# Reading a weight-mixing stage's bases two at a time, 8 KB to a partition

## The chip, the cores and the metric

The kernel runs on one core of a Trainium2 chip. The metric is the device time of one execution in microseconds (us). The core has five engines that run side by side and wait for each other by semaphores: TensorE (PE in the profile; its weight loads are PEld), VectorE (DVE), ScalarE (ACT), GpSimd (POOL) and SyncE (SP). SP and POOL also issue the DMA transfers, which the core's 16 DMA engines carry out.

## The reference

Two layers of a graph network with 625 nodes of 512 features. The change lies in the first of the two graph convolutions of the first layer, in one einsum:

```python
def rgcn_gate_layer(x, row, col, edge_type, basis, att, gate_w, root, bias):
    w = jnp.einsum('rb,bio->rio', att, basis)      # att [2, 30], basis [30, 512, 512]
    x_j = x[col]
    msgs = []
    for r in range(NUM_RELATIONS):                 # 2 relations
        gate = jax.nn.sigmoid(x_j @ gate_w[r, :, 0])
        msgs.append(gate[:, None] * x_j @ w[r])
    msg = jnp.where((edge_type == 0)[:, None], msgs[0], msgs[1])
    agg = jax.ops.segment_sum(msg, row, num_segments=x.shape[0])
    return agg + x @ root + bias

h = jax.nn.relu(rgcn_gate_layer(x, row, col, edge_type, basis1, att1, gate_w1, root1, bias1))
out = rgcn_gate_layer(h, row, col, edge_type, basis2, att2, gate_w2, root2, bias2)
```

So 30 bases of 512 x 512 numbers in f32 (31.5 MB) are summed into two weight matrices, one for each relation, with 30 factors each. The second convolution does the same with its own 30 bases. Around these stand a linear attention, expert layers and, in the second layer, graph attentions.

## The kernel before, in words

**Mixing layer one's bases on TensorE.** `mix_bases_1` builds 32 steps `q`, each a pair of functions, `load` and `step`. The bases are in two groups of 15 (`BGROUPS`); the even `q` take the first group, the odd ones the second, and each two consecutive `q` cover 32 rows `i` of the bases. `loaded` (L320) takes a tile `basis` of 128 partitions x 4 x 512 from a pool of three (`basis_pool`), and issues four transfers on SP (L325). Transfer j brings 8 rows (`BROWS`) of each of 15 bases into column block j: partition 8b + c holds row c of base b, so 120 partitions are filled with 2 KB each. `step` (L328) then runs four matrix products (L334), one for each column block. Their stationary operand is `att1[g]`, 120 x 32, which holds att in the places (8b + c, 2c + r): the product sums over the bases and puts row c, relation r into PSUM row 2c + r. Four blocks fill the four quarters of one PSUM bank, the second group is added to the first, ACT copies the bank to `stage` (L338), and POOL issues four stores (L341) from `stage` into `wmix`, the mixed weights, with 8 partitions x 2 relations x 512 each.

**The order of work.** It is written out by hand: inside `manual_schedule`, PE and SP run in program order. `mix(n)` loads and runs n steps. The program starts with two steps; then for each group of 11 edge columns (`count_group`, one-hot products on PE that count edges) it runs one or two steps and one piece of the linear attention (`key`, `value`, `query`), and after the last group come the steps left over. The last four steps alternate with the first slices of layer two (the string `plan`, `DPDPDPDP` and then D's): a "D" loads three quarters of one base of layer two into a tile of the same pool (L356 on SP) and DVE adds it with its factor (L367). The first quarter of each of layer two's bases comes through `ring`, loaded by POOL's queue (L356), and is added by DVE. `load_w` (L79) brings `wk`, `wv`, `wq` and `root` on SP in between. When the last step of layer one is done, `root_products(1)` and `root_products(3)` run, and then `messages(1, ...)` multiplies the nodes with `wmix` (L138).

**Transfers.** SP's transfers use eight semaphores in turn, and one that reuses a semaphore waits until the transfer before it on that semaphore has landed.

Of the kernel before, what the change touches and what calls it, by code (L numbers as in the profile page):

```python
# [21 lines left out]
D = 512  # L22
# [6 lines left out]
BROWS = 8  # L29
# [16 lines left out]
def kernel(ctx: ExitStack, tc: tile.TileContext, A, out: bass.AP):  # L46
    nc = tc.nc
# [126 lines left out]
    def mix_bank():  # L174
        return banks[2]()
# [135 lines left out]
    def mix_bases_1(wpool):  # L311

        w = wpool.tile([128, 2, KD * D], F32, name="wmix")
        src = A["L0_gnn_basis1"].rearrange("b (i c) o -> i b c o", c=BROWS)
        acc = [None]

        def loaded(q):  # L320
            i0, g = 4 * (q // 2), q % 2
            n, b0 = BGROUPS[g], sum(BGROUPS[:g])
            bt = basis_pool.tile([128, KD, D], F32, name="basis")
            for j in range(4):
                nc.sync.dma_start(bt[:BROWS * n, j, :], src[i0 + j, b0:b0 + n])  # L325
            return bt

        def step(q, bt):  # L328
            i0, g = 4 * (q // 2), q % 2
            k = BROWS * BGROUPS[g]  # L330
            if g == 0:
                acc[0] = mix_bank()
            for j in range(4):
                nc.tensor.matmul(acc[0][32 * j:32 * j + 32, :], att1[g][:k], bt[:k, j, :],  # L334
                                 start=(g == 0), stop=(g == 1))
            if g == 1:
                sg = stage_pool.tile([128, D], F32, name="stage")
                nc.scalar.copy(sg, acc[0])  # L338
                for j in range(4):
                    k, p0 = (i0 + j) // 16, 8 * ((i0 + j) % 16)  # L340
                    nc.gpsimd.dma_start(w[p0:p0 + 8, :, k * D:(k + 1) * D], sg[32 * j:32 * j + 16, :])  # L341

        return w, [(lambda q=q: loaded(q), lambda bt, q=q: step(q, bt)) for q in range(32)]

    class Added:
# [91 lines left out]
    b0 = 0  # L437
    for n in BGROUPS:
        k = BROWS * n
# [19 lines left out]
    for i in range(2):  # L459
        g = rowsA.tile([128, KD, 32], F32, name=f"gwp{i}")  # L460
# [46 lines left out]
    def gates_of(psg):  # L507
        gate = rowsA.tile([P, NT, 2], F32, name="gate")
        nc.scalar.activation(gate.rearrange("p t r -> p (t r)"), psg[:P, :2 * NT], AF.Sigmoid)
        return gate  # L510

    wm1, steps = mix_bases_1(wpool)

    def mix(n=1):
# [1066 lines left out]
```

## Time and profile before

| | |
|---|---|
| median of three runs | 981.48 us (976.95 to 981.51) |
| the profiled execution: its time, its span | 975.78 us, 974.0 us |
| busy: PE, DVE, ACT, POOL | 890.9, 514.2, 304.1, 142.8 us |
| basis transfers of layer one (L325) | 128 of 240 KB, from 3.3 to 215.4 us |
| products on them (L334) | 256, of which 224 in `mix` banks, 650 ns each |
| end of the last of these products | 221.8 us |

The span runs from the first to the last instruction; the run's time is a little longer. The times of the profile's views are counted from the start of the span. In the page, a group of instructions is named by its line, its engine, its operation and its tiles (output<-inputs). "Busy" of PE includes pipelined matrix products, so a busy PE is not PE at its peak. The DMA share is the mean busy share of the 16 DMA engines, and a transfer is cut into packets, of which each belongs to one engine.

### The profile page before, as it was taken

What the parts mean: (1) busy time and instruction counts of PE and PEld (TensorE: products, weight loads), DVE (VectorE), ACT (ScalarE), POOL (GpSimd) and SP (SyncE); (2) the same over time, 40 slices, a digit from 0 to 9 for tenths busy, and PEclk for the clock granted to TensorE, in tenths of its full rate; (3) what the DMA queues carried; (4) which work ended last, traced back from release to release, by engine and by line L of the source; (5) the groups of instructions that cost most, each with busy time, mean ns of one, the idle gap of its engine ahead of it and who ended that gap; (6) DMA issues with size and microseconds to landing.
All of it is one profiled execution on the core that took longest, in us unless ns stands there. A gap on an engine that the chain in (4) does not pass through costs nothing. (4 is left out here: it accounts for less than half of the span.)

```text
span 974.0 us, 10135 instructions
## 1 busy us (share of the span) xinstructions
PE 890.9 (91%) x3606; PEld 488.1 (50%) x3606; DVE 514.2 (53%) x980; ACT 304.1 (31%) x508; POOL 142.8 (15%) x223
## 2 busy tenths in 40 slices
PE   3898899979999999789969999999988899997997
PEld 1333234534474448767735655555544554444543
DVE  7778694566889723422254632233355754566320
ACT  2566475611120021111125432322243442311310
POOL 6644231110000200330020000000000000011310
PEclk9999999999999999799989999999999999997999
DMA  8899997575487920889831111212210104020001
GB/s 243 244 280 259 251 248 185 169 196 196 135 285 230 334 87 2 265 292 331 281 120 56 44 43 47 81 46 87 86 64 27 61 1 128 10 77 2 0 6 47
DMA packets 70842, 135.06 MB, mean 139 GB/s; under 512 B 9298, under 2 KB 11485, under 8 KB 70787
## 3 DMA queue, kind: packets, MB, share of 16 engines
q1 hardware_dynamic: 61554, 114.19, 38.3%
q0 software_dynamic: 9232, 20.16, 6.9%
q8 instruction: 31, 0.51, 0.2%
q14 instruction: 25, 0.20, 0.1%
HBM read 123.37 MB, written 8.85 MB: 136 GB/s over the span
## 5 line engine op out<-in xcount | busy, mean ns | idle before, releaser
L367 DVE SCALAR_TENSOR_TENSOR wmix<-basis,att,wmix 128x1536 f32<-128x1536 f32 x58 | 101.4, 1811 | 12.8 <-DMA basis<-in_L_gnn_basis_dram 12.8
L133 PE MATMUL ps<-y1T,wh 128*128 128x512 f32 (+1 forms) x256 | 74.5, 440 | 1.5 <-DVE hm L1281 1.0
L138 PE MATMUL ps<-hm,wh 128*128 128x512 f32 (+1 forms) x256 | 71.7, 433 | 0.0
L233 DVE TENSOR_SCALAR os<-iota,edges,wbits 125x626 bf16<-125x626 f16 x123 | 49.9, 469 | 26.6 <-PE tail L236 26.5
L138 PE MATMUL ps<-wmix,xnT 128*125 128x512 f32 x140 | 61.9, 592 | 0.0
L235 PE MATMUL main<-os,odg 125*128 125x512 bf16 x165 | 48.7, 381 | 11.9 <-ACT os L231 6.4
L133 PEld LDWEIGHTS ps<-y1T,wh 128*128 128x128 f32 x256 | 41.1, 190 | 33.8 <-issue 30.6
L138 PEld LDWEIGHTS ps<-hm,wh 128*128 128x128 f32 x256 | 39.7, 191 | 30.7 <-issue 30.7
L341 POOL DMA_DIRECT2D wmix<-stage x64 | 37.0, 581 | 98.2 <-ACT stage L338 98.1
L334 PE MATMUL mix<-basis,att 120*32 120x512 f32 x224 | 42.4, 650 | 8.8 <-DVE att L450 5.6
L659 PE MATMUL ps<-z,counts 125*125 125x512 f32 x200 | 48.3, 397 | 0.6 <-PEq L644 0.6
L1291 DVE TENSOR_TENSOR acc<-acc,sg 128x625 f32<-128x625 f32 x15 | 12.2, 811 | 64.1 <-ACT sg L1289 64.1
L367 DVE SCALAR_TENSOR_TENSOR w<-ring,att,w 128x512 f32<-128x512 f32 x58 | 40.8, 752 | 9.8 <-DMA ring<-in_L_gnn_basis_dram 9.8
L1281 DVE TENSOR_SCALAR hm<-ps,bh 128x625 f32<-128x625 f32 x32 | 27.7, 867 | 31.4 <-PE ps L133 31.4
L138 PEld LDWEIGHTS ps<-wmix,xnT 128*125 128x125 f32 x140 | 26.3, 188 | 33.8 <-issue 33.0
L1279 ACT ACTIVATE hm<-ps,bh 128x625 f32<-128x625 f32 x32 | 25.0, 782 | 55.4 <-PE ps L133 55.4
L138 PEld LDWEIGHTS ps<-xgT,w1e 128*128 128x128 f32 x320 | 38.1, 199 | 7.7 <-ACT xgT L1021 7.7
L659 PEld LDWEIGHTS ps<-z,counts 125*125 125x125 f32 x200 | 36.5, 185 | 10.8 <-issue 2.2
L138 PE MATMUL ps<-xgT,w1e 128*128 128x128 f32 x320 | 39.9, 285 | 1.2 <-ACT xgT L1021 1.2
L138 PE MATMUL ps<-w2e,hTe 128*128 128x512 f32 x80 | 37.5, 595 | 3.0 <-DVE hTe L1030 3.0
L636 ACT ACTIVATE z<-ps,gate 125x512 fp32r<-125x512 f32 x20 | 13.7, 687 | 79.9 <-PE ps L138 79.9
L133 PE MATMUL ps<-xnT,wq 128*128 128x113 f32 (+1 forms) x128 | 36.5, 438 | 2.0 <-DVE cT L74 1.2
(358 smaller groups left out, 1522.6 us busy)
## 6 DMA issues: line engine op xcount, KB each, us to landing
basis<-in_L_gnn_basis_dram SPq DMA_DIRECT2D x128, 240.0 KB
basis<-in_L_gnn_basis_dram SPq DMA_DIRECT2D x30, 768.0 KB
w1e<-in_L_ffn_W_dram SPq DMA_DIRECT2D x10, 1024.0 KB
w2e<-in_L_ffn_W_dram SPq DMA_DIRECT2D x10, 1024.0 KB
ring<-in_L_gnn_basis_dram POOLq DMA_DIRECT2D x30, 256.0 KB, 7.9
wh<-in_L_gnn_Wh_dram SPq DMA_DIRECT2D x4, 1024.0 KB
xd<-stage POOLq DMA_DIRECT2D x12, 256.0 KB, 6.4
b2row<-in_L_ffn_b_dram SPq DMA_DIRECT2D x10, 256.0 KB
```

The costliest lines, as they stand in the source:

```text
L133: nc.tensor.matmul(ps[:m, lo:hi], l, r[:, lo:hi], start=(i == 0), stop=(i == len(pairs) - 1))
L138: nc.tensor.matmul(ps, l, r, start=(i == 0), stop=(i == len(pairs) - 1))
L233: nc.vector.tensor_scalar(os_, iota, edges[:, 0, c:c + 1], wfield[:, c:c + 1], op0=OP.is_equal, op1=OP.mult)
L235: nc.tensor.matmul(main0, od[:, c - c0, :], os_[:, :BANK], start=c == 0, stop=c == NE - 1)
L334: nc.tensor.matmul(acc[0][32 * j:32 * j + 32, :], att1[g][:k], bt[:k, j, :], start=(g == 0), stop=(g == 1))
L341: nc.gpsimd.dma_start(w[p0:p0 + 8, :, k * D:(k + 1) * D], sg[32 * j:32 * j + 16, :])
L367: nc.vector.scalar_tensor_tensor(w[:, r, :], self.tiles[b], c, w[:, r, :], op0=OP.mult, op1=OP.add)
L636: nc.scalar.activation(hi[:, t, :], ps[:P], AF.Copy, scale=g)
L659: nc.tensor.matmul(ps[:P], l, r, start=first and i == 0, stop=last and i == len(pairs) - 1)
L1279: nc.scalar.activation(hm[:, m, :], ps[:, :N], AF.Relu, bias=b)
L1281: nc.vector.tensor_scalar(hm[:, m, :], ps[:, :N], b, 0.0, op0=OP.add, op1=OP.max)
L1291: nc.vector.tensor_add(acc, acc, sg)
```

## The change

A transfer brings two bases instead of fifteen, and 32 neighbouring rows of each instead of 8. Row 4c + i of the 32 lies in partition c, block i, so that a partition gets four neighbouring rows, 8 KB in one piece. Two bases fill 16 partitions; seven such transfers and one of a single base fill the tile's 120 partitions. The tile's shape, the pool, the products and their operand stay. Block j now holds the rows 4c + j in place of 8j + c, so the stores put the mixed rows into every fourth partition.

```diff
-        src = A["L0_gnn_basis1"].rearrange("b (i c) o -> i b c o", c=BROWS)
+        src = A["L0_gnn_basis1"].rearrange("b (q c i) o -> q b c i o", c=BROWS, i=4)
         acc = [None]
 
         def loaded(q):
-            i0, g = 4 * (q // 2), q % 2
+            g = q % 2
             n, b0 = BGROUPS[g], sum(BGROUPS[:g])
             bt = basis_pool.tile([128, KD, D], F32, name="basis")
-            for j in range(4):
-                nc.sync.dma_start(bt[:BROWS * n, j, :], src[i0 + j, b0:b0 + n])
+            for b in range(0, n, 2):
+                m = min(2, n - b)
+                nc.sync.dma_start(bt[BROWS * b:BROWS * (b + m)], src[q // 2, b0 + b:b0 + b + m])
             return bt
 
         def step(q, bt):
-            i0, g = 4 * (q // 2), q % 2
+            g = q % 2
             k = BROWS * BGROUPS[g]
...
             if g == 1:
                 sg = stage_pool.tile([128, D], F32, name="stage")
                 nc.scalar.copy(sg, acc[0])
+                k, p0 = q // 8, 32 * (q // 2 % 4)
                 for j in range(4):
-                    k, p0 = (i0 + j) // 16, 8 * ((i0 + j) % 16)
-                    nc.gpsimd.dma_start(w[p0:p0 + 8, :, k * D:(k + 1) * D], sg[32 * j:32 * j + 16, :])
+                    nc.gpsimd.dma_start(w[p0 + j:p0 + 32:4, :, k * D:(k + 1) * D], sg[32 * j:32 * j + 16, :])
```

## The prediction

> **What bounds the kernel now.** I read the windows view by stage first, then the waits of the first 222 us, then the basis tile's rows, and last the DMA view of two short stretches, because the change only re-cuts transfers.
>
> ```profile
> 50.00:100.00 50.00, 44.21 (x221) 17.55 (x221) 41.47 (x75) 31.36 (x43) 19.49 (x38) 0.97 1.00 270
> 100.00:150.00 50.00, 44.88 (x210) 17.30 (x204) 38.93 (x68) 27.23 (x38) 15.94 (x27) 1.00 0.99 250
> ```
>
> After the window come its length, then busy time of PE, PEld, DVE, ACT, POOL, granted clock, DMA share and GB/s. In the stage that mixes layer one's bases all 16 DMA engines are taken (share 1.00), at 250 to 270 GB/s, and PE is busy nine tenths of the time. So both are close to being the bound here. After 222 us the bases of layer one are done and PE carries the end (91% of the span).
>
> ```profile
> SPq L325 <- PE mix L334: 44.5, 12, 6.8
> SPq L325 <- DMA basis<-in_L_gnn_basis_dram: 22.8, 20, 5.6
> PEld mix L334 <- DMA basis<-in_L_gnn_basis_dram: 15.9, 19, 2.7
> PEld ps L334 <- DMA basis<-in_L_gnn_basis_dram: 9.3, 7, 2.5
> PE ps L334 <- DMA basis<-in_L_gnn_basis_dram: 6.2, 5, 3.0
> PE mix L334 <- DMA basis<-in_L_gnn_basis_dram: 3.1, 4, 1.8
> ```
>
> Total, times, longest, in the first 222 us. TensorE and its weight loads stood 34.5 us (15.9 + 9.3 + 6.2 + 3.1) for a basis tile: that is the most that better transfers could win. SP's queue is not full: it waits for a free buffer or for a transfer to land.
>
> ```profile
> L325 SPq DMA_DIRECT2D basis<-in_L_gnn_basis_dram x128: 835/838/1225, 3.3 to 215.4; - x128
> L356 SPq DMA_DIRECT2D basis<-in_L_gnn_basis_dram x30: 367/368/563, 179.5 to 320.7; - x30
> ```
>
> Issue time on SP in ns (least, median, most). A transfer whose source counts in two steps (15 bases, 8 rows) and whose tile counts in one (120 partitions) costs SP 838 ns; one whose two sides count alike costs 368.
>
> How many of the 16 engines does one transfer use? The DMA view of 115.2 to 120.8 us, where basis transfers alone move data, tells:
>
> ```profile
> DMA packets 816, 1.49 MB, mean 266 GB/s; under 512 B 90, under 2 KB 90, under 8 KB 816
> q1 hardware_dynamic: 816, 1.49, 99.0%
> basis<-in_L_gnn_basis_dram SPq DMA_DIRECT2D x6, 240.0 KB
> ```
>
> 726 packets carry rows; at 120 rows each that is 6.05 transfers. The other 90 packets are small, 14.9 for a transfer: I read them as one closing packet from each engine that took part, so fifteen engines carry a transfer whose source has 15 outermost steps. The stretch of 803 to 816 us shows what a transfer on few engines does:
>
> ```profile
> DMA  0002350332422333333333333333333300004967
> DMA packets 640, 1.27 MB, mean 98 GB/s; under 512 B 20, under 2 KB 20, under 8 KB 640
> bb<-in_L_gnn_b_dram SPq DMA_DIRECT2D x1, 250.0 KB
> bb_b<-in_L_gnn_bsk_dram SPq DMA_DIRECT2D x1, 250.0 KB
> g<-in_L_gnn_g_dram SPq DMA_DIRECT2D x1, 250.0 KB
> be<-in_L_gnn_be_dram SPq DMA_DIRECT2D x1, 250.0 KB
> ```
>
> Four rows are loaded into 125 partitions, issued within 1.5 us of each other. They end with 20 small packets, five each: 5 is the largest number up to 16 that divides 125. And the DMA line stays at 3 tenths, 5 of 16 engines, for ten microseconds: the four do not spread over the idle eleven engines, they queue on the same five. What one engine gives:
>
> ```profile
> 689.50:692.00 2.50, 2.50 (x10) 1.34 (x9) 0.87 (x1) 0.38 (x1) 0.00 (x0) 1.00 0.32 131
> 808.00:813.00 5.00, 5.00 (x13) 2.19 (x12) 2.19 (x4) 0.58 (x1) 1.27 (x1) 1.00 0.33 128
> ```
>
> Last two columns: share and GB/s, both on five engines; the first has rows of 4 KB, the second of 2 KB. That is 26.2 and 25.6 GB/s an engine. Row size is worth 2%, no more.
>
> **The change, part by part.**
>
> *The loads.* The bytes stay: 32 tiles of 120 rows of 8 KB, 31.5 MB. Four transfers of 240 KB for a tile become seven of 128 KB (two bases) and one of 64 KB (the fifteenth basis). In a pair the source, read from `src[q // 2, b0 + b:b0 + b + m]`, counts 2 bases, then 8 stretches of 8 KB; the tile counts 16 partitions. The Trainium skill ("DMA: Bandwidth & Descriptors", section "Why a DMA increments its semaphore by 16 and not by 1") says that a transfer is split along the outermost count of each side, over the largest number of engines up to 16 that divides both, and that on the hardware queues these are the lowest-numbered ones. The rows above agree as far as they reach (15 for 15 and 120; 5 for 125 and 125, always the same five), but 15 also follows from the 120 partitions alone, so no row here tells "both sides" from "the partitions". By the partitions a pair would use 16 engines and lose nothing; by both sides it uses **2**, and 224 pairs queue behind one another on the same two engines while fourteen idle. I take 2, as the rule is stated for both sides and nothing in the trace contradicts it.
>
> Then the stage is bound by those two. Each carries half of every pair, 224 x 64 KB = 14.68 MB, and one row of each single (8 partitions, 8 engines), 32 x 8 KB = 0.26 MB: 14.94 MB at 25.6 GB/s is 584 us. They also carry their sixteenth of all else that moves meanwhile: the ring slices of layer two 7.9 MB, four weight loads 4.2, four slices of 768 KB 3.1, the wmix stores 2.1, x 0.8: 18.1 MB / 16 = 1.13 MB, 44 us. The sum is 628 us from the first issue at 3.3 us: the last tile lands at about 631 us.
>
> The same skill page ("Why small descriptors are slow") charges each packet some 3 fixed cycles beside one for each 32 bytes: 67 for 64 at 2 KB, 259 for 256 at 8 KB, so 8 KB rows would run 3.4% faster. The trace's 2% from 2 to 4 KB is of that size. By the rule the 584 us become 565; with the measured 2 KB rate 584. I keep 584 and let the rule set the low end.
>
> *SP's issues.* 256 instead of 128. A pair still counts differently on its two sides, so between 368 and 838 ns, and I take 838: 224 x 0.838 + 32 x 0.34 (a row load with equal sides, the 281 to 294 ns of `bb` at the end and up) = 199 us, against 107 now. Spread over 628 us this lies beside the transfers and costs nothing; if the transfers were quick it would fill the stage (rival two). Behind SP's waiting loads stand `wk`, `wv`, `wq`, `root` and the first `slices` loads, in program order, so these come late as well, but their users on PE (`key`, `value`, `query`, root_products) stand between mix steps that wait longer. POOL's `ring` loads meet the same two engines with a sixteenth of their rows, and DVE's `w20` steps wait for that; 18 us a tile cover it.
>
> *TensorE.* Before, product j of a tile needed transfer j alone; now each needs all eight. The last tile's four products (593 ns each) then run one after another behind the last landing, where now one does: 2 us later than before. Elsewhere they hide in the wait: a tile takes 7 x 2.56 = 18 us to arrive (64 KB at 25.6 GB/s each), and PE was busy 182.6 us of 12 to 221 us, about 6 us for each of the 32 tiles.
>
> *The way back.* ACT's copy is unchanged; the four `wmix` stores from POOL have the same count, bytes and shape (8 partitions, 2 rows of 2 KB), with a partition step of 4. Nearest row: 550 ns of issue, 6.7 us to land. Bounds: a microsecond less or more for each landing; they have 37 us between groups, and the last four lie beside the 7.5 us of root products:
>
> ```profile
> 220.73 1.04 PE L334 MATMUL ps<-basis,att 120*32 120x512 f32 x2 [0.51 <-DMA basis<-in_L_gnn_basis_dram]
> 229.49 1.02 PE L138 MATMUL ps<-wmix,xnT 128*125 128x512 f32 x2
> ```
>
> I take 0, range -1 to +2 us.
>
> *What comes after.* The last product of layer one's bases ends at 221.8 us now; 752 us follow, nearly all PE, in the same order, with the slices of layer two loaded on all 16 engines as before. Only what precedes the last tile waits.
>
> **The sum.** 631 + 3 (landing, products) + 752 = 1386 us of span, 1388 with the 1.8 us that lie between this execution's span (974.0) and its time (975.78). The median of the runs shown, 981.48, is 0.6% above the profiled one; I don't add that.
>
> **The rivals.**
>
> *Two engines (chance 0.87).* The forecast. Its own range: 27 GB/s an engine and 30 us of other traffic give 1342; 24 GB/s, 47 us and 10 us of gaps between tiles give 1440.
>
> *Sixteen engines, SP the bound (0.07).* Should the split follow the partitions, 199 us of basis issues and some 6 us of others must pass through SP before the last tile, of 215 us that pass now, with hardly a wait allowed. Each wait for a buffer then adds: 975 to 1010, say 985. Against it: the rule; for it: 838 ns where counts differ.
>
> *The stage gets shorter (0.06): faster.* One mechanism: enough engines and issues at 368 ns. Layer one's 31.5 MB need 144 GB/s to keep the present 218 us, which at 25.6 is six engines; from there on the split costs nothing, and 8 KB rows give back half of the 34.5 us of waits: about 960. The point that decides is the number of engines a pair uses: under six it loses, above it wins.
>
> **How the numbers follow.** The two-engine case holds 0.87 and ends slower. Of the second 0.01 is faster, 0.02 same, 0.04 slower; all of the third is faster. About 0.5% (5 us) is what a measurement of this kernel can tell from no change. That makes 0.07, 0.02 and 0.91. The range 1335 to 1440 holds nearly all of the two-engine case and leaves the others out.
>
> **What would show it.** Right: from 5 to about 630 us the DMA line at 1 to 2 tenths (2 of 16 is 0.13, plus ring and slices) and near 60 GB/s; PE at a third or less of busy time there; waits of L334 for basis of hundreds of us; 3,840 rows of 8 KB in q1 in place of 15,360 of 2 KB; after it the old 752 us. Wrong: a DMA share above 0.4 in the stage means more engines; an SPq without waits means the issue bound; an L325 median near 368 would spoil the 838.

## The result and the profile after

The changed kernel takes 1416.76 us (median of four runs, 1415.68 to 1419.91) against 979.22 us for the kernel before on the same chip: 1.4475 times as long, with a 95% interval of 1.442 to 1.4529. The forecast was 1388 us, in a range of 1335 to 1440. The span of the profiled execution is 1413.9 us, of which TensorE is busy 932.6 us (890.9 before).

The first view is part 2 of the page after: the span in 40 slices of 35.3 us, with the busy tenths of PE, the granted clock, the mean share of the DMA engines and what they moved.

```profile
PE   0203332343335353614999989979999998999798
PEclk9855556666577685756999989989999999999899
DMA  3442211112111113324378158841122220031001
GB/s 112 129 142 81 82 57 58 56 58 79 58 58 59 58 55 97 91 73 140 130 270 300 62 159 288 298 153 60 30 60 60 89 75 30 30 89 59 1 1 37
```

Slices 6 to 15 (176 to 530 us) stand at one tenth and 55 to 59 GB/s, but for one of 79 in which a weight also arrives: for 350 us the transfers keep little more than two of the sixteen engines busy. PE works about a third of that time, and from slice 20 (from 670 us) it runs as before. The windows view (length, busy PE, PEld, DVE, ACT, POOL, granted clock, DMA share, GB/s) gives the same for two stretches, and the DMA view for the second of them:

```profile
200.00:250.00 50.00, 15.36 (x57) 5.15 (x58) 5.05 (x10) 6.95 (x10) 2.22 (x4) 0.60 0.15 57
250.00:300.00 50.00, 18.61 (x75) 7.06 (x73) 9.69 (x19) 11.77 (x16) 2.22 (x4) 0.67 0.15 57
```

```profile
DMA packets 515, 2.84 MB, mean 57 GB/s; under 512 B 154, under 2 KB 154, under 8 KB 186
q1 hardware_dynamic: 386, 2.69, 13.4%
basis<-in_L_gnn_basis_dram SPq DMA_DIRECT2D x19, 128.0 KB
basis<-in_L_gnn_basis_dram SPq DMA_DIRECT2D x2, 64.0 KB
```

In 50 us SP's queue moved 2.69 MB. Two singles are in it, whose rows go to eight engines, so about 0.1 MB of theirs went to other engines than the first two. The rest, 2.59 MB in 50 us on two engines, is about 26 GB/s an engine, at the 25.6 to 26.2 that the two stretches of before gave.

The kernel feels it as one wait. Three rows of the waits of the first 680 us (engine, tile, line, what it waited for: us in total, times, longest), one of SP's queue, and the row of the basis tile's loads (issue time on SP in ns, least, median, most):

```profile
PE mix L336 <- DMA basis<-in_L_gnn_basis_dram: 352.7, 27, 27.3
DVE os L233 <- PE tail L236: 331.9, 14, 37.0
...
PE ps L336 <- DMA basis<-in_L_gnn_basis_dram: 59.4, 4, 18.3
```

```profile
SPq L327 <- DMA basis<-in_L_gnn_basis_dram: 428.8, 208, 4.3
```

```profile
L327 SPq DMA_DIRECT2D basis<-in_L_gnn_basis_dram x256: 278/605/4835, 3.3 to 636.4; - x128
```

(L325, L334 and the like of before are two lines further down here; in some experiments they are one or three.) PE stands 412 us (352.7 + 59.4) for bases, where PE and its weight loads together stood 34.5 us before. SP stands 428.8 us for earlier transfers to land, so its own issuing holds nothing up. DVE's 331.9 us are only handed on, as the edge counts wait for PE, and PE for the bases between them. The end of the stage, in the timeline of PE:

```profile
657.12 1.93 PE L336 MATMUL ps<-basis,att 120*32 120x512 f32 x8 [18.29 <-DMA basis<-in_L_gnn_basis_dram]
...
659.46 4.05 PE L661 MATMUL ps<-root,xnT 128*125 128x512 f32 x8
...
667.43 4.88 PE L138 MATMUL ps<-wmix,xnT 128*125 128x512 f32 x11
```

The messages begin at 667.43 us, against 229.49 before. What follows takes 746.5 us here and 744.5 there. All of the loss but 2 us lies ahead of that point.

### The profile page after: what moved, and what is told of

The parts are those of the page before. It is cut to its first block, busy times and chain, and to the rows that moved or that the text cites. A ratio compares the mean times of both kernels' runs of the same rounds, so it can differ in the third digit from the quotient of the medians.

```text
span 1413.9 us, 10434 instructions
## 1 busy us (share of the span) xinstructions
PE 932.6 (66%) x3606; PEld 502.0 (36%) x3606; DVE 512.0 (36%) x980; ACT 303.6 (21%) x508; POOL 138.6 (10%) x223
## 2 busy tenths in 40 slices
DMA packets 58108, 135.09 MB, mean 96 GB/s; under 512 B 8081, under 2 KB 10268, under 8 KB 54210
## 5 line engine op out<-in xcount | busy, mean ns | idle before, releaser
L336 PE MATMUL mix<-basis,att 120*32 120x512 f32 x224 | 54.2, 1059 | 352.7 <-DMA basis<-in_L_gnn_basis_dram 352.7
L233 DVE TENSOR_SCALAR os<-iota,edges,wbits 125x626 bf16<-125x626 f16 x123 | 47.2, 446 | 332.2 <-PE tail L236 331.9
L336 PEld LDWEIGHTS mix<-basis,att 120*32 120x32 f32 x224 | 6.2, 140 | 375.2 <-issue 207.5
L138 PE MATMUL ps<-hm,wh 128*128 128x512 f32 (+1 forms) x256 | 71.7, 433 | 0.0
L340 ACT COPY stage<-mix 128x512 f32<-128x512 f32 x14 | 8.2, 585 | 291.7 <-PE mix L336 258.0
L138 PE MATMUL ps<-wmix,xnT 128*125 128x512 f32 x140 | 61.9, 592 | 0.0
L138 PEld LDWEIGHTS ps<-hm,wh 128*128 128x128 f32 x256 | 39.7, 191 | 30.7 <-issue 30.7
L336 PE MATMUL ps<-basis,att 120*32 120x512 f32 x32 | 7.7, 1058 | 59.4 <-DMA basis<-in_L_gnn_basis_dram 59.4
L138 PE MATMUL ps<-wk,xnT 128*125 128x512 f32 x80 | 43.8, 700 | 0.0
L138 PE MATMUL ps<-wv,xnT 128*125 128x512 f32 x80 | 42.6, 683 | 0.0
L133 PE MATMUL ps<-xnT,wq 128*128 128x113 f32 (+1 forms) x128 | 40.1, 468 | 1.9 <-DVE cT L74 1.1
L661 PE MATMUL ps<-root,xnT 128*125 128x512 f32 x80 | 40.0, 647 | 0.8 <-DMA root<-in_L_gnn_root_dram 0.8
L138 PE MATMUL ps<-w2e,hTe 128*128 128x512 f32 x80 | 38.4, 607 | 2.4 <-DVE hTe L1032 2.4
L138 PEld LDWEIGHTS ps<-xgT,w1e 128*128 128x128 f32 x320 | 37.3, 195 | 7.5 <-ACT xgT L1023 7.5
```

What stands on the lines that cost most here:

```text
L133: nc.tensor.matmul(ps[:m, lo:hi], l, r[:, lo:hi], start=(i == 0), stop=(i == len(pairs) - 1))
L138: nc.tensor.matmul(ps, l, r, start=(i == 0), stop=(i == len(pairs) - 1))
L233: nc.vector.tensor_scalar(os_, iota, edges[:, 0, c:c + 1], wfield[:, c:c + 1], op0=OP.is_equal, op1=OP.mult)
L661: nc.tensor.matmul(ps[:P], l, r, start=first and i == 0, stop=last and i == len(pairs) - 1)
```

## The experiments

Theory: a transfer is split along the outermost count of both sides, over the largest number of engines up to 16 that divides both, so a pair uses two engines and layer one's bases need their time. Rivals: the split follows the partitions and SP's issues bind; or the long rows or the whole-tile waits cost the time; or the order of work on DVE, which the scheduler rearranged, does.

One table first, by which all runs can be read. "Small" is the count of packets under 512 bytes in part 2 of each page. The other transfers have 7,377 or 7,378 of them in every kernel here, and the rest are the closing packets of layer one's transfers, read as in the prediction as one for each engine taking part. On that reading the number of engines can be counted; it comes out whole for every kernel, and the 2 of the changed kernel agrees with its rate above. "Start" is the first product on `wmix` (L138), and "after it" the span less that.

| kernel | layer one's transfers | small packets | engines | start, us | after it | time, us |
|---|---|---|---|---|---|---|
| before | 128 | 9,298 = 7,378 + 128 x 15 | 15 | 229.5 | 744.5 | 979.22 |
| after | 224 + 32 | 8,081 = 7,377 + 224 x 2 + 32 x 8 | 2 | 667.4 | 746.5 | 1416.76 |
| e1 rows outermost | 224 + 32 | 9,425 = 7,377 + 256 x 8 | 8 | 326.5 | 746.7 | 1073.99 |
| e2 three bases | 160 | 7,857 = 7,377 + 160 x 3 | 3 | 494.0 | 749.5 | 1245.27 (one run) |
| e3 five bases | 96 | 7,857 = 7,377 + 96 x 5 | 5 | 350.7 | 749.8 | 1102.29 (one run) |
| e4 fifteen bases | 32 | 7,857 = 7,377 + 32 x 15 | 15 | 256.2 | 745.4 | 1002.42 |
| e9 two halves | 64 | 8,337 = 7,377 + 64 x 15 | 15 | 239.8 | 747.7 | 988.94 |
| e12 issues doubled | 256 | 11,217 = 7,377 + 256 x 15 | 15 | 261.5 | 743.7 | 1006.46 |

The times without a mark are medians of four or more runs. The kernel before ran beside each group of experiments with a median of 977 to 979 us. No kernel here beats it.

**e1: the same pairs, rows outermost.** Only the order of the source's counts differs from the changed kernel: the same 224 pairs into the same 16 partitions, with the same 8 KB rows. The rows of a pair now lie in a different order in the partitions, so the operand `att` is built to match.

```diff
-                nc.sync.dma_start(bt[BROWS * b:BROWS * (b + m)], src[q // 2, b0 + b:b0 + b + m])
+                nc.sync.dma_start(bt[BROWS * b:BROWS * (b + m)],
+                                  src[q // 2, b0 + b:b0 + b + m].rearrange("b c i o -> c b i o"))
```

> The transfers of the changed kernel with their 16 rows in another order: the same two bases, the same 16 partitions and rows of 8 KB, 224 pairs and 32 singles on SP, but the source counts 8 row stretches first and 2 bases second (partition 2c + b in place of 8b + c; the mixing operand is permuted to match). Two-engine theory (the outermost count of the source sets the engines): 8 engines a pair, 31.46 MB / (8 x 26.2 GB/s) = 150 us, so transfers no longer bind; SP's 224 issues at 0.6 to 0.84 us (135 to 188 us) come near the stage's 218: 975 to 1010 us, DMA share in the stage above 0.4. Rival, 16 partitions or small transfers are slow in themselves: no change from 1417. Rival, SP's queue is the bound with 256 issues: no change from 1417.

Measured: 1073.99 us (1068.35 to 1079.5), 1.0993 times before (1.0921 to 1.1065). The windows view of e1:

```profile
150.00:200.00 50.00, 41.45 (x185) 15.80 (x184) 19.61 (x39) 23.85 (x33) 10.43 (x19) 0.86 0.58 194
```

The share is 0.58 where it was 0.23 in the changed kernel at the same place. With partitions, bytes, row length and number of transfers alike, 343 us go away: the outermost count of the source decides, 8 rows outermost giving eight engines and 2 bases giving two, both against 16 partitions. A split by the partitions alone would leave nothing to win here. That the tile's side counts too is not shown: in every load of layer one's bases here the tile's partitions are a multiple of the source's count. But 97 us over the kernel before are more than was expected. Two lines of its waits, DVE's timeline around them, and the first `ring` loads of POOL in e1 and in the kernel before:

```profile
PE main L235 <- DVE os L233: 62.8, 2, 41.8
...
DVE w L368 <- DMA ring<-in_L_gnn_basis_dram: 26.5, 1, 26.5
```

```profile
23.67 1.61 DVE L224 TENSOR_TENSOR odg<-iota,dmod 125x1408 bf16<-125x1408 f16 x1
51.80 0.88 DVE L368 TENSOR_SCALAR w<-ring,att 128x512 f32<-128x512 f32 x2 [26.52 <-DMA ring<-in_L_gnn_basis_dram]
52.60 4.72 DVE L370 SCALAR_TENSOR_TENSOR w<-ring,att,w 128x512 f32<-128x512 f32 x7
57.24 3.27 DVE L233 TENSOR_SCALAR os<-iota,edges,wbits 125x626 bf16<-125x626 f16 x9
```

```profile
44.72 2.18 POOL L359 DMA_DIRECT2D ring<-in_L_gnn_basis_dram  x4
```

```profile
15.03 1.09 POOL L356 DMA_DIRECT2D ring<-in_L_gnn_basis_dram  x2
```

PE waits 62.8 us for the one-hot tiles `os` of the edge counts, because DVE's queue holds additions of layer two's ring slices ahead of them, and the first of these waits 26.5 us for its data. Only PE and SP run in written order. The order on DVE is the scheduler's, and it came out otherwise for the new transfers: 9 of the 60 ring additions went ahead of the second group's `os` operations, and the other 51 ahead of the third's. POOL's order came out otherwise too. It issues the first `ring` load only at 44.72 us, behind two chains of small operations on biases (those that use `three_rows`), where before it began at 15.03, so the data that DVE waits for is late from there. In the kernel before PE's wait for `os` is 5.5 us (six times, longest 1.6). This was in no step of the prediction; e5 to e8 look into it.

**e2 and e3: three and five bases to a transfer.**

```diff
-            for b in range(0, n, 2):
-                m = min(2, n - b)
+            for b in range(0, n, 3):      # e3: 5
+                m = min(3, n - b)         # e3: 5
```

> Three bases in a transfer in place of two, nothing else: 160 transfers of 192 KB, 24 partitions. Two-engine theory: three engines, 31.46 MB / 3 / 26.2 GB/s = 400 us for the bases; with the changed kernel's 81 us of other traffic and gaps, 6 us ahead and 757 us behind: 1246 us. If the number of transfers counts (2.5 us each, as 256 took about 640): 6 + 400 + 757, about 1165 us.

> Five bases in a transfer: 96 transfers of 320 KB, 40 partitions, five engines. Two-engine theory: 31.46 MB / 5 / 26.2 = 240 us, plus 49 to 81 us for other traffic and gaps: 6 + 289 to 321 + 757 + 2 = 1054 to 1086 us. If the number of transfers counts: 6 + 240 + 757, about 1005 us.

Measured: 1245.27 and 1102.29 us, one run each. Their windows, e2 first:

```profile
150.00:200.00 50.00, 26.36 (x119) 10.38 (x117) 15.22 (x30) 18.16 (x25) 2.34 (x5) 0.80 0.21 82
```

```profile
150.00:200.00 50.00, 32.60 (x150) 12.60 (x148) 18.48 (x37) 21.54 (x30) 6.55 (x12) 0.80 0.41 141
```

With three engines the time is within 1 us of the sum that was given, one engine's rate times three with the changed kernel's other traffic and gaps added, at a share of 0.21. With five it is 16 us above the range given. There the engines no longer bind alone, as SP's queue and PE's waits show:

```profile
SPq L327 <- PE mix L336: 113.0, 23, 25.8
```

```profile
PE main L235 <- DVE os L233: 50.7, 3, 21.4
```

SP waits 113 us for PE to free a buffer, and PE 50.7 us for DVE's `os` tiles, the wait that e1 shows. Either can hold up the loads: whole tiles in three buffers, or the order on DVE. How much of the 16 us belongs to which was not separated. (e2 has 45.3 us of the second wait too; there the three engines hide it.)

**e4 and e9: all fifteen engines, long rows.** e4 loads a tile in one transfer of 960 KB with 8 KB rows; e9 in two of 480 KB with 4 KB rows. Both keep the changed kernel's order of rows and its stores to every fourth partition.

```diff
-            for b in range(0, n, 2):
-                m = min(2, n - b)
+            for b in range(0, n, 15):
+                m = min(15, n - b)
```

> All fifteen bases in one transfer: 32 transfers of 960 KB, rows of 8 KB, fifteen engines as before the change, and a quarter of its issues. Two-engine theory: the transfers no longer bind as they did, rows of 8 KB save 2 to 4% of their time and SP issues 27 us in place of 107; all four products of a tile now wait for the whole tile. 965 to 985 us, within 1.5% of the kernel before. Rival, the 8 KB layout itself (four rows to a partition, stores to every fourth partition) is what costs: well above 1000 us.

Measured: 1002.42 us (997.5 to 1004.56), 1.0256 times before (1.0207 to 1.0305). The expectation was wrong: longer rows on the same engines, and a quarter of the issues, made it slower.

```profile
100.00:150.00 50.00, 36.22 (x181) 14.21 (x180) 33.33 (x58) 24.05 (x34) 15.72 (x26) 0.90 0.98 238
```

```profile
DVE w L369 <- DMA ring<-in_L_gnn_basis_dram: 42.2, 13, 14.2
...
PE main L235 <- DVE os L233: 25.1, 10, 10.7
```

```profile
ring<-in_L_gnn_basis_dram POOLq DMA_DIRECT2D x30, 256.0 KB, 11.2
```

The engines are as full as before (0.98 against 0.99), and move 238 GB/s where 2 KB rows moved 250 in the same stretch. DVE waits 42.2 us for ring tiles (its row before: 9.8 us, four times, longest 4.3), and PE 25.1 us for DVE (before: 5.5). A ring load lands 11.2 us after its issue (median; 7.9 before). DVE's order in this stage is that of the kernel before. I read it as the 960 KB in front of a ring slice on the same engines holding it back. If so, halves should give back about half of the loss:

```diff
-                nc.sync.dma_start(bt[BROWS * b:BROWS * (b + m)], src[q // 2, b0 + b:b0 + b + m])
+            for j in (0, 2):
+                nc.sync.dma_start(bt[:BROWS * n, j:j + 2], src[q // 2, b0:b0 + n, :, j:j + 2])
```

> Two transfers for a tile, each with two of the four rows of all fifteen bases (480 KB, rows of 4 KB, 15 engines); the changed kernel's layout otherwise. If the whole-tile wait costs e4 its 25 us, half of it comes back: 985 to 995 us. If rows of 4 KB and a quarter less waiting outweigh it: below 975, and the version to keep. If e4's loss is the scheduler's order alone: no relation, 970 to 1010.

Measured: 988.94 us (985.53 to 990.82), 1.0114 times before (1.0066 to 1.0162). The loss falls with the size of a transfer, from 25 to 11 us. Three rows of e9, its waits and its ring loads, say what is left:

```profile
PE main L235 <- DVE os L233: 5.1, 5, 2.2
...
PEld mix L335 <- DMA basis<-in_L_gnn_basis_dram: 24.7, 12, 4.0
```

```profile
ring<-in_L_gnn_basis_dram POOLq DMA_DIRECT2D x30, 256.0 KB, 9.2
```

PE's wait for DVE is back at the 5.5 us of before, but PE and its weight loads stand 51.5 us for bases, counted as in the prediction, where it was 34.5 before and 40.2 in e4. By these waits, most of e4's loss came through the ring, and what e9 still loses comes at the products that wait for half a tile. That supports the reading for e4, and does not prove it, as rows and whole-tile waits change with the size. The layout, which e9 shares, can then hardly cost more than e9's 11 us.

**e5 to e8: the order on all engines fixed.** Here all five engines run in the written order in the first stage, so the loads cannot move anything. The chains that use `three_rows` had to go to later places for that.

```diff
-    in_order = tc.manual_schedule(engines={mybir.EngineType.PE, mybir.EngineType.SP})
+    in_order = tc.manual_schedule(engines={mybir.EngineType.PE, mybir.EngineType.SP, mybir.EngineType.DVE,
+                                           mybir.EngineType.Activation, mybir.EngineType.Pool})
```

e5 is the kernel before with this, e6 is e1, e7 is e4, and e8 is the changed kernel.

> The kernel before, with DVE, ACT and POOL of the first stage also held to one written order (and the two three_rows chains put at the groups g == 2 and g == 5), so that the scheduler can't reorder them when the transfers change. It is the base for the three kernels sent with it. Either theory: 965 to 1000 us.

> Pairs of bases with the 8 row stretches counted first (8 engines), in that fixed order. If the 97 us that e1 lost came from the scheduler's putting the w20 additions ahead of the edge counting on DVE: within 25 us of e5. If it came from 8 engines or from 256 issues on SP: still 60 to 100 us above e5.

> One transfer of fifteen bases for a tile, in that fixed order. If e4's 25 us came from the scheduler's order: within 8 us of e5. If they come from products that wait for a whole tile (rows of 8 KB): 20 to 30 us above e5.

> The changed kernel in that fixed order. Two-engine theory: the two engines stay busy from 6 to about 650 us whatever DVE does, so 1395 to 1417 us: the order is worth 20 us at most. If the order were the cause of the loss: near e5.

Measured: e5 1052.72 us (1.0758 times before, 1.0679 to 1.0837), well outside the 965 to 1000 expected, e6 1102.25 (1.1274, 1.1192 to 1.1356), e7 1070.61 (1.0936, 1.0856 to 1.1017), e8 1417.9 (one run). The waits of e5 and e6:

```profile
PE main L235 <- DVE os L233: 67.3, 10, 14.8
...
DVE w L367 <- DMA ring<-in_L_gnn_basis_dram: 18.6, 8, 12.8
```

```profile
PE main L235 <- DVE os L233: 85.2, 11, 21.3
...
DVE w L370 <- DMA ring<-in_L_gnn_basis_dram: 40.1, 12, 18.6
```

The kernel before loses 74 us to the written order and the moved chains alone, so this was a poor instrument: it puts the very wait that it should remove into every kernel. What it still shows: with all orders alike, e1's cut costs 50 us over e5 (97 with the scheduler's order), between the two expectations, and e4's costs 18 us over e5 (25 otherwise). That suggests that part of e1's 97 us is the order and part is not; with PE's wait for `os` at 67.3 us in one and 85.2 in the other, the split is not settled. The changed kernel is another matter: 1417.9 against 1416.76 us. With two engines binding, the order on DVE is worth nothing that shows, though the scheduler rearranged it in the changed kernel too.

**e10 and e11: the pairs spread over two queues.** Of each tile, the first, third, fifth and seventh pair stay on SP, and the three others and the single go to ACT's queue (e10) or POOL's (e11).

```diff
-                nc.sync.dma_start(bt[BROWS * b:BROWS * (b + m)], src[q // 2, b0 + b:b0 + b + m])
+                (nc.scalar if b % 4 else nc.sync).dma_start(bt[BROWS * b:BROWS * (b + m)], src[q // 2, b0 + b:b0 + b + m])
```

> The changed kernel with 96 of its 224 pairs and the singles issued from ACT's queue in place of SP's. Two-engine theory: both queues hand pairs to the same two engines, so nothing is gained: 1400 to 1440 us, stage DMA share 0.15 to 0.2. If SP's queue were the bound: SP has 128 issues left, about 1420 - 0.43 x 430 = 1235 us or less.

> The same 96 pairs and the singles from POOL's queue. If POOL's transfers go to other engines than the first two (a pair of engines that moves on), the first two keep 128 pairs, 8.4 MB, and a sixteenth of the rest: 9.2 MB / 26.2 GB/s = 350 us, plus 81, 6 ahead and 757 behind: about 1195 us. If they too go to the first two: 1417 us.

Measured: 1411.45 and 1224.52 us, one run each. The issues of e10, then its window and that of e11:

```profile
L327 ACTq DMA_DIRECT2D basis<-in_L_gnn_basis_dram x128: 277/620/1264, 0.8 to 631.6; - x128
```

```profile
250.00:300.00 50.00, 20.97 (x82) 7.79 (x83) 7.11 (x15) 8.37 (x12) 2.18 (x4) 0.65 0.15 57
```

```profile
100.00:400.00 300.00, 145.89 (x649) 58.55 (x647) 106.23 (x198) 86.15 (x136) 89.33 (x162) 0.72 0.38 108
```

Two queues that issue side by side move the same 57 GB/s at the same share, 0.15: ACT's pairs go to the same two engines as SP's, so neither SP's issue rate nor the depth of its queue is the bound. POOL's pairs go to other engines, at least for the most part: with all pairs on the same two the time would have stayed near 1417 us, and 192 us come back, 30 fewer than the estimate for that case (1195). The share of 0.38 overstates it, since 27 of the 30 ring loads fall into that window too.

**e12: twice the issues, fifteen engines.** The kernel before with each of its four transfers cut in two halves of the columns: 256 transfers of 120 KB, as many as the changed kernel has, with unlike counts and rows of 1 KB.

```diff
-                nc.sync.dma_start(bt[:BROWS * n, j, :], src[i0 + j, b0:b0 + n])
+                for o in (0, 256):
+                    nc.sync.dma_start(bt[:BROWS * n, j, o:o + 256], src[i0 + j, b0:b0 + n, :, o:o + 256])
```

> The kernel before with each of its transfers cut into two column halves: 256 transfers of 120 KB on fifteen engines, rows of 1 KB, issues on SP as many as in the changed kernel. It prices 256 issues alone. At 0.84 us an issue SP is full (215 us of the 218): 1000 to 1040 us. If issues were free: 975 to 990 us (1 KB rows cost a little). In neither case near 1417.

Measured: 1006.46 us (1005.51 to 1010.08), 1.0307 times before (1.0244 to 1.037). Its basis tile's row and SP's waits of the first 260 us:

```profile
L326 SPq DMA_DIRECT2D basis<-in_L_gnn_basis_dram x256: 835/836/1552, 3.3 to 249.7; - x128
```

```profile
SPq L326 <- PE tail L236: 8.3, 11, 0.9
SPq L326 <- DMA basis<-in_L_gnn_basis_dram: 4.7, 7, 1.4
SPq L326 <- PE mix L335: 4.3, 6, 0.9
```

256 issues of 836 ns are 214 us of the 247 us that they span, and only 17 us of waits are left: SP is nearly full, which is rival two, and it goes with 29 us. Rows of 1 KB may have a part in that. The number of transfers, then, explains at most a fifteenth of the changed kernel's 438 us.

## Why the prediction was right

**Two engines for a pair.** Right, and the step that carried it. The rule of both sides was taken from the Trainium skill ("DMA: Bandwidth & Descriptors", section "Why a DMA increments its semaphore by 16 and not by 1"), while the trace of before could not tell it from a split by the partitions. Now the runs do: the count of closing packets is 2 for a pair, 8 for the same pair with its rows outermost, and 3, 5 and 15 in e2 to e4. They would be the same if the source alone decided, which no run here tells apart.

**The bases' 584 us.** Nearly right, 20 us too high. In the stretch of 286 to 299 us pairs alone move data:

```profile
DMA packets 95, 0.69 MB, mean 53 GB/s; under 512 B 11, under 2 KB 11, under 8 KB 11
```

That is 26.5 GB/s an engine, at which the 14.94 MB take 564 us. The Trainium skill ("DMA: Bandwidth & Descriptors", section "Why small descriptors are slow"), with some 3 fixed cycles for each packet, would have made 8 KB rows 3.4% quicker than 2 KB rows and the term 565 us, an estimate that the prediction set aside. On these two engines it comes out (26.5 against 25.6 GB/s), while with all engines full e4 moved less than before.

**Everything else on the two engines: 44 us.** This is the term that was mis-sized. Rows of 8 KB passed from 5.7 to 656.6 us, 651 us, where 628 was the sum: less 564, the rest is 87 us, twice the forecast. That only 23 us of this show is luck, as the bases' term erred the other way. A part can be named: in the first 657 us 51.9 MB moved, which is 20.5 MB beside layer one's 31.5, where the prediction counted 18.1. At a sixteenth each and 25.6 GB/s that is 50 us in place of 44. By the packets in the trace, no row of 8 KB was under way for 14 us in all, 5 of them in stretches of over 0.2 us; some of these may hold other traffic. The other 23 or so are not assigned.

**The last tile and what comes after.** Right: the last eight products end 2.4 us after the last row, for 3 forecast, and 754.9 us follow them, for 752. One of the root groups beside the last stores took 4.05 us instead of 3.60, in a stretch of low clock. The stores of `wmix` every fourth partition cost nothing that shows, as forecast.

**SP.** 224 issues at 838 ns were forecast; a pair costs 605. Without effect on the time, since SP waited 428.8 us in any case.

**The signs named.** DMA at 1 to 2 tenths, near 60 GB/s, PE at about a third, hundreds of us of waits and 3,840 long rows in place of the short ones: all there (58,108 - 54,210 = 3,898 packets of 8 KB or more, 58 of them the instruction queues' own). The misses add up as follows: those 23 us (43 more for the rest, 20 less for the bases) and the 2.4 from the first issue to the first row, which the sum had at nothing; 0.6 less for the last products; 3 more after them; and 1 by which the median lies above the profiled execution. That is the 29 us between 1388 and 1416.76.

**The rivals.** Sixteen engines with SP as the bound fell with e10 and e12, the shorter stage with the two engines. More engines would not have brought it either: the prediction put the point from which the split costs nothing at six, but e1 lost 97 us on eight, in part it seems through the order on DVE, and even on fifteen, longer rows and fewer transfers were 1.1 to 2.6% slower (e9, e4). What neither the forecast nor a rival held is the scheduler's new order on DVE and POOL. Here it hides behind the two engines (e8). In a version that keeps more engines busy, as e1 does, it comes to light (62.8 us of PE's waits).

## What to carry to other kernels

When a transfer is re-cut, write down the outermost count on both sides: a source that counted 2 outermost had two engines, however many partitions it filled. The longest row is no use to a transfer on two engines, and issuing it from a second queue may land on the same two. For transfers from SP's and ACT's queues the closing packets in the profile, counted against the number of transfers, give the engines; for POOL's the count does not work (e11 has 20,689 packets under 512 bytes, which leaves 102 for each of POOL's 128 basis transfers). Where the engines were full already, longer rows and larger transfers won nothing here, and the small urgent loads beside them landed later; and after any change of transfers, look at whether an engine that is not in written order has been rearranged.

## What was not expected of the hardware

TensorE's granted clock fell with its work: 0.55 to 0.76 in the windows from 50 to 657 us of the changed kernel, 0.60 at 200 to 250 us where PE was busy 15 of 50 us. A mix product took 1,059 ns on average there, against 650 before. Here it costs almost nothing, since PE waits anyhow, and from 660 to 700 us, with PE busy throughout, it is 1.00 again.

SP's time for issuing a transfer whose two sides count unlike goes with the cut: median 605 ns with two engines, 701 with three, 709 with five, 666 in e1 with eight, and 836 to 839 with fifteen (rows of 1 to 8 KB). ACT's queue needed 620 (median of its 96 pairs and 32 singles).
